# Moving VectorE's side work behind the PSUM sums in a fused modulated-convolution kernel

## The chip, the cores and the metric

The kernel runs on one core of a Trainium2 chip. The metric is the device time of one execution in microseconds (us). The engines are TensorE (PE in the profile; PEld is its weight load), VectorE (DVE), ScalarE (ACT), GpSimd (POOL) and SyncE (SP), which issues the DMAs here. Every engine works through its own instructions in the order in which the program gives them.

## The reference, cut to what matters

A batch of 128 sequences of 64 channels and 1024 positions goes through four modulated 1-D convolutions in a row, with a residual at the end. Each layer has its own style-dependent weights per sample:

```python
TYPES = ('same', 'upsample', 'same', 'downsample')
def _layer(x, style, w, b, mw, mb, typ):
    s = style @ mw.T + mb                                  # (B, 64)
    weight = SCALE * w * s[:, None, :, None]               # per-sample filter, K = 3
    demod = lax.rsqrt(jnp.sum(weight * weight, axis=(2, 3)) + EPS)
    weight = weight * demod[:, :, None, None]
    ...                                                    # conv, bias, blur with [1,3,3,1]
out = x
for i, typ in enumerate(TYPES):
    out = _layer(out, style, weights[i], biases[i], mod_w[i], mod_b[i], typ)
return x + out
```

All four layers are linear in x, so away from the ends of the sequence one sample's result is one convolution with nine taps of 64x64, plus a constant. All data are float32.

## The kernel before, in words

The kernel builds the nine-tap filter of each sample on the chip and applies it once. The 128 partitions hold two samples of 64 channels, a pair p (64 pairs). One iteration q of the main loop handles four samples, the pairs p = 2q and 2q + 1; there are NQ = 32 iterations. The order of all engines' work is written out by hand in this loop, and the semaphores follow from the order in the text.

**Filters.** For the samples of iteration c = q + 2, `stage2(c)` and `stage3(c, 0)`, `stage3(c, 1)` run on TensorE (psR and psW in the profile), and `stage1(q + 3)` (psS) one iteration further ahead. ScalarE copies their results from PSUM, scaled (S, R, Wf, and wd in `scale3`). `combine(c)` on VectorE then makes the filters H from Wf (lines 460 to 473); h1 and h2, complete with line 472, are what the first products of iteration c need.

**Convolution.** The nine taps are applied in three groups of three by a fast filtering scheme: five products m0 to m4 in place of nine. The input of a pair, X, is stored as three planes. From it come five combined inputs, the slots of tile T:
- `pre1(p)`: two VectorE instructions make G from X (lines 499 and 504), and two POOL instructions make T1 and T2 from G (510 and 511); it also issues a load of X;
- `pre2(p)`: `pre2a` makes T3 from X (line 522, VectorE) and issues the other load of X, `pre2b` makes T0 and T4 together from G ("T04", line 532, VectorE).

`convA12(p)` and `convA3(p)` are the products m1, m2 and m3 into PSUM (psA); ScalarE copies m1 out (`copy_m1`, line 573). `seed(p)` consists of `seed1(p)`, the sums u, v and y1, and `seed2(p)`, the two sums that are written into the PSUM banks Y; all are on line 585, read PSUM and run on VectorE. `convB(p)` adds m0 and m4 to Y on TensorE. `output(p, s)` scales Y and y1 into the tile o on ScalarE (line 642), in the last iterations in part on VectorE and POOL (644), and `store(p, s)` sends it off through SP. Y is one pair of banks, so `seed2` of a pair waits until the outputs of the pair before have been read; pairs 61 and 63 have banks of their own (Y2). psA has two buffers.

**Side work.** The three columns at each end of every sequence, and the scale and bias vectors of the samples after the first 16 (`PART[1]`, `REST`), are computed piece by piece alongside. Matrix products of it stand in `SLOTS` (psE, copied to `raw` by ScalarE), the rest in the table `EXTRA`, whose entry (q, 0) belongs to the first half of iteration q and (q, 1) to the second. Most entries are a few short VectorE instructions; (2, 1) is

```python
        (2, 1): lambda: (var_root(REST, after(0)), const_rest(1, PART[1], after(1))),
```

of which `var_root` has an ACT instruction (nw, line 231) and a VectorE one (var, line 232) and `const_rest` two VectorE ones (cc, lines 732 and 733). (2, 0), (4, 1) and (5, 0) are POOL work alone, (3, 0), (4, 0) and (6, 0) have some (lines 270 to 273, 679 to 686). (25, 0) ends with the store of the ends, `out_ends`.

Of the kernel before, what the change touches and what calls it, by code (L numbers as in the profile page):

```python
# [63 lines left out]
def kernel(  # L64
# [12 lines left out]
    NQ = B // 4  # L77
# [86 lines left out]
    def y_bank(p, s):  # L164
        return Y2[p][s] if p in Y2 else Y[:, s]

    def zeros_to_y(sets, n, p=0):


        for i in range(sets):  # L170
            rows = HALF[i % 2]
            for cols in HALF:
                nc.tensor.matmul(
                    y_bank(p, i % 2)[cols, :n], Z[rows, :C], Z[rows, :n], start=True, stop=True
                )
# [53 lines left out]
    def var_root(bs, src, ls=slice(0, NL)):  # L229
        src = by_layer(src, bs)[:, ls]  # L230
        nc_a.activation(nw[:, ls, bs], src, AF.Sqrt, bias=eps)
        nc_v.tensor_scalar(var[:, ls, bs], src, EPS, None, op0=ALU.add)

    def var_inverse(bs, ls=slice(0, NL)):
        nc_v.reciprocal(dm[:, ls, bs], nw[:, ls, bs])
# [14 lines left out]
    def var_newton(bs, ls=slice(0, NL)):  # L250

        newton(var[:, ls, bs], dm[:, ls, bs], nw[:, ls, bs])
# [26 lines left out]
    def table_B(bs):  # L279
        table(nc_g, tB, bs, ALT, DOWN, sc[:, 2, bs], sc[:, 1, bs])  # L280

    def table_0(bs):
        table(nc_g, t0, bs, ALT, ODD, sc[:, 0, bs], 1.0)
# [235 lines left out]
    def pre2a(p, eng=nc_v):  # L519
        if p < NP:  # L520
            X, t = Xs[p % NX], Ts[p]
            eng.tensor_sub(t[:, 4, :NJ], plane(X, 3), plane(X, 1))  # L522
            load(p + NX, slice(1, 3))

    def pre2b(p):
        if p >= NP:
            return
        t, g = Ts[p], Gs.pop(p)

        a, b = plane(g, 2), plane(g, 0)  # L530
        both = lambda v, step: bass.AP(v.tensor, v.offset, [list(v.ap[0]), [step, 2], [1, NJ]])
        nc_v.tensor_sub(t[:, 0:2, :NJ], both(a, PL), both(b, 1))  # L532

    def pre2(p):
        pre2a(p)
        pre2b(p)
# [22 lines left out]
    def m_tile(tag, p, shape=(2, NB)):  # L559
        return mpool.tile([P, *shape], F32, tag=tag, name=f"{tag}_{p}")  # L560
# [23 lines left out]
    def sum_of(out, x, f, y):  # L584
        nc_v.scalar_tensor_tensor(out, x, f, y, op0=ALU.mult, op1=ALU.add)  # L585

    def seed1(p):
        if p >= NP:
            return
        m1, m2, m3 = part.pop(p)  # L590
        u, v = m_tile("u", p), m_tile("v", p)
        y1s[p] = mpool.tile([P, 2, NB], F32, tag="y1", name=f"y1_{p}", bufs=3)
        sum_of(u, m2, -1.0 / 3.0, m1)
        sum_of(v, m2, 1.0 / 3.0, m1)
        sum_of(y1s[p], m3, 2.0 / 6.0, v)
        part[p] = m3, u

    def seed2(p):
        if p >= NP:
            return  # L600
        m3, u = part.pop(p)
        banks = [(slice(s, s + 1), y_bank(p, s)[:, None]) for s in range(2)]
        if p not in Y2:
            banks = [(slice(0, 2), Y)]
        for i, f in enumerate((1.0 / 6.0, 4.0 / 6.0)):
            for k, y in banks:
                sum_of(y[..., i * NB : (i + 1) * NB], m3[:, k], f, u[:, k])

    def seed(p):
        seed1(p)  # L610
        seed2(p)
# [14 lines left out]
    def convB(p, between=None):  # L626
        product(p, 0, [y_bank(p, s)[:, :NB] for s in range(2)])
        if between:
            between()
        product(p, 4, [y_bank(p, s)[:, NB : 2 * NB] for s in range(2)])  # L630
        Ts.pop(p)
        os[p] = opool.tile([P, 2, HO], F32, tag="o", name=f"o{p}")
# [45 lines left out]
    def vector_a1(bs):  # L678
        nc_g.tensor_mul(a1[:, bs], sc[:, 2, bs], sc[:, 1, bs])
# [11 lines left out]
    def vector_b1(bs):  # L691
        with_bias(b1s, sc[:, 2], 1, bs)
# [32 lines left out]
    def const_rest(l, bs, src):  # L725
        src = src[:, : bs.stop - bs.start]
        if l == 2:
            nc_v.tensor_mul(oc[:, bs], src, dm[:, 3, bs])
            nc_v.tensor_scalar(oc[:, bs], oc[:, bs], bb[:, 3:4], None, op0=ALU.add)
        else:  # L730
            add, f = ((b1s, 2.0), (c2f, 1.0))[l]
            nc_v.tensor_mul(cc[l][:, bs], src, (a1, Da)[l][:, bs])
            nc_v.scalar_tensor_tensor(
                cc[l][:, bs], add[:, bs], f, cc[l][:, bs], op0=ALU.mult, op1=ALU.add
            )
# [12 lines left out]
    def zeros():  # L748
        for t in Ye:
            nc_g.memset(t[:, :, 0:1], 0.0)  # L750
            nc_g.memset(t[:, :, 7:8], 0.0)
        for t in Ue:
            nc_g.memset(t[:, :, 0:1], 0.0)
            nc_g.memset(t[:, :, 10:11], 0.0)
        for t in Ve:
            nc_g.memset(t[:, :, 0:2], 0.0)
            nc_g.memset(t[:, :, 10:12], 0.0)
        nc_g.memset(g1, 0.0)
# [255 lines left out]
    def after(side):  # L1014
        return raw[turn[0]][:, side, :]

    def layers(i, j):
        return REST, slice(i, j)


    EXTRA = {
        (1, 1): lambda: const_rest(0, PART[1], after(0)),
        (2, 0): lambda: (table_B(REST), vector_a1(REST)),
        (2, 1): lambda: (var_root(REST, after(0)), const_rest(1, PART[1], after(1))),
        (3, 0): lambda: (var_inverse(*layers(2, 3)), table_0(REST), vector_b1(REST)),
        (3, 1): lambda: (
            const_rest(2, PART[1], after(0)),
            var_newton(*layers(2, 3)),
            var_inverse(*layers(1, 2)),
# [32 lines left out]
        (24, 1): rest3,  # L1062
        (25, 0): rest3_bias,
    }
    for q in range(NQ):
        p = 2 * q
        c, s = q + 2, q + 3
        if q == 1:
            nc.sync.dma_start(Xe, x_ends)
        if q == 5:  # L1070
            zeros()
        if c < NQ:
            stage2(c)
        convB(p)
        output(p, 0)

        if c < NQ:
            stage3(c, 0)
        if q < NQ - 1:
            output(p, 1)  # L1080
        else:
            output(p, 1, nc_v, ((0, 2),))
            output(p, 1, nc_g, ((2, 3),))
            store(p, 0)
            store(p, 1)

            convB(p + 1)
            for i, j, engs in ((2, 3, (nc_a, nc_g)), (0, 2, BOTH)):
                for r, eng in enumerate(engs):
                    output(p + 1, r, eng, ((i, j),))  # L1090
                    store(p + 1, r, slice(i * NB, j * NB))
            break
        convA12(p + 2)
        if q > 2:
            pre1(p + 4)
            store(p, 0)
            seed(p + 1)
            store(p, 1)
            pre2(p + 3)
        elif q:  # L1100

            seed(p + 1)
            pre2(p + 3)
            store(p, 0)
            pre1(p + 4)
            store(p, 1)
        else:
            store(p, 0)
            store(p, 1)
            seed2(p + 1)  # L1110
            var_inverse(PART[1])
            var_newton(PART[1])
            table_A(PART[1], dm[:, 2, PART[1]])
            for of in (table_C, vector_c0, table_3, vector_Da):
                of(PART[1])
            pre2(p + 3)
            pre1(p + 4)
        EXTRA.get((q, 0), lambda: None)()
        if c < NQ:
            stage3(c, 1)  # L1120
        convA3(p + 2)
        if q == NQ - 2:
            convA12(p + 3)
            copy_m1(p + 3)
        side = SLOTS.get(q)
        convB(p + 1, (lambda: slot(*side)) if side else None)
        output(p + 1, 0)
        if q == NQ - 2:
            seed(p + 2)
            convA3(p + 3, lambda p: None)  # L1130
            output(p + 1, 1, nc_v, ((0, 2),))
            output(p + 1, 1, nc_g, ((2, 3),))
            seed_last(p + 3)
        else:
            output(p + 1, 1)
        if c == NQ - 1:

            banks = unit(ps_w, "Y2")
            Y2[p + 3] = Y2[p + 5] = banks
            zeros_to_y(2, 2 * NB, p + 3)  # L1140
        if q > 2 and q < NQ - 2:
            pre1(p + 5)
        if q < NQ - 2:
            seed(p + 2)
        if s < NQ:
            stage1(s)
        if s + 1 < NQ:
            scale3(s + 1)
        if c < NQ:
            combine(c)  # L1150
        pre2(p + 4)
        store(p + 1, 0)
        if q < 3:
            pre1(p + 5)
        store(p + 1, 1)
        EXTRA.get((q, 1), lambda: None)()
        if q < NQ - 2:
            convA12(p + 3)
            convA3(p + 3)
# [74 lines left out]
```

## Time and profile before

| | |
|---|---|
| median of 3 runs | 501.93 us (499.55 to 502.47) |
| own time of the profiled execution | 499.52 us |
| span of the profiled execution | 497.7 us |
| TensorE busy | 486.4 us, 98% of the span |
| VectorE busy | 440.6 us, 89% |
| ScalarE busy | 324.6 us, 65% |
| GpSimd busy | 134.3 us, 27% |

The span runs from the first to the last instruction of the program on the core; the device time of the same execution is 1.8 us longer. A profile's row gives an instruction's line in the kernel, its engine, operation and tiles; a timeline row begins with its start and its duration in us. Ends of matmuls are modelled, and some matmul records are missing after 180 us. One full iteration lasts some 14.4 us, longer where `SLOTS` adds products.

### The profile page before, as it was taken

To read this page: it belongs to the slowest core of one execution; us is meant where nothing else is said; L and a number is where in the kernel's file an instruction comes from. 1 tells how busy PE (TensorE), PEld (TensorE's weight loads), DVE (VectorE), ACT (ScalarE), POOL (GpSimd) and SP (SyncE) were. 2 spreads that over 40 slices of the span, in tenths; PEclk is the share of its full clock that TensorE was granted. 3 is DMA by queue.
4 is the path that set the end of the run, shared out by engine and by line. 5 is a ranking of instruction groups with operands and counts; after the bars stand their busy time and mean duration, and the time that the engine had idled before them with its cause. 6 is when DMAs were issued, how large, how long until landed. Compare 5 with 4: busy or idle time off the path is not lost.

```text
span 497.7 us, 28344 instructions
## 1 busy us (share of the span) xinstructions
PE 486.4 (98%) x12600; PEld 475.7 (96%) x12600; DVE 440.6 (89%) x926; ACT 324.6 (65%) x796; POOL 134.3 (27%) x198
## 2 busy tenths in 40 slices
PE   8999999999999999999999999999999999999985
PEld 5899998999999999999999999999999999999985
DVE  5888989999999889987979998879999889988895
ACT  5456767567767667767667667657667657766642
POOL 4143224254312212212212222212212212221210
PEclk9999999999999999999999999999999999999999
DMA  7132654535554425553435554425555435554223
GB/s 251 61 89 88 212 141 136 153 109 172 164 166 146 141 81 170 172 162 118 135 107 172 168 163 145 150 70 172 173 158 144 139 86 184 172 173 131 92 96 129
DMA packets 37610, 70.81 MB, mean 142 GB/s; under 512 B 4208, under 2 KB 29040, under 8 KB 37488
## 3 DMA queue, kind: packets, MB, share of 16 engines
q1 hardware_dynamic: 37408, 68.88, 44.8%
q8 instruction: 99, 1.62, 1.4%
q14 instruction: 23, 0.19, 0.1%
q10 hardware_dynamic: 80, 0.11, 0.1%
HBM read 35.36 MB, written 33.62 MB: 139 GB/s over the span
## 4 chain that ended last, share of the span: by engine, by line
PE 74%; DVE 3%; ACT 0%; issue 0%
PE psA L550 25%; PE Y L550 18%; PE psR L393 13%; PE psW L430 11%; PE psS L362 5%; PE psE L792 2%; DVE Y L585 1%; ACT o L642 0%; DVE T L532 0%; DVE G L499 0%; DVE v L585 0%; DVE T L522 0%; DVE u L585 0%; DVE o L644 0%; DVE H L472 0%
## 5 line engine op out<-in xcount | busy, mean ns | idle before, releaser
L550 PE MATMUL psA<-T,H 64*64 64x170 f32 x4608 | 207.1, 304 | 2.1 <-DVE Y L585 1.8
L550 PEld LDWEIGHTS psA<-T,H 64*64 64x64 f32 x4608 | 190.2, 133 | 2.7 <-POOL o L644 2.1
L510 POOL TENSOR_TENSOR T<-G 128x342 f32<-128x342 f32 x62 | 56.9, 918 | 319.3 <-DVE G L504 211.5
L550 PE MATMUL Y<-T,Wf 64*64 64x170 f32 x3072 | 141.4, 304 | 1.6 <-DVE Y L585 1.6
L550 PEld LDWEIGHTS Y<-T,Wf 64*64 64x64 f32 x3072 | 128.8, 133 | 3.1 <-ACT m L573 1.4
L642 ACT ACTIVATE o<-Y,oc,dm 128x340 f32<-128x340 f32 x125 | 79.6, 637 | 56.3 <-PE Y L550 56.1
L430 PE MATMUL psW<-R,par 64*64 64x256 f32 (+3 forms) x1536 | 100.1, 349 | 0.0
L585 DVE SCALAR_TENSOR_TENSOR Y<-psA,u 128x340 f32<-128x340 f32 (+1 forms) x132 | 66.5, 508 | 35.9 <-ACT o L642 33.5
L393 PE MATMUL psR<-S,E 64*64 64x192 f32 (+1 forms) x2304 | 94.1, 299 | 1.2 <-DVE S L342 1.0
L340 ACT ACTIVATE Wf<-psW,t 128x256 f32<-128x256 f32 (+1 forms) x252 | 75.5, 382 | 23.1 <-PE psW L430 23.1
L430 PEld LDWEIGHTS psW<-R,par 64*64 64x64 f32 x1536 | 86.0, 133 | 3.0
L393 PEld LDWEIGHTS psR<-S,E 64*64 64x64 f32 x2304 | 86.8, 133 | 1.8 <-DVE S L342 1.3
L340 ACT ACTIVATE R<-psR,tC 128x448 f32<-128x448 f32 x63 | 36.6, 631 | 57.5 <-PE psR L393 54.7
L642 ACT ACTIVATE o<-y,oc,dm 128x170 f32<-128x170 f32 x125 | 65.8, 527 | 0.0
L499 DVE SCALAR_TENSOR_TENSOR G<-X 128x688 f32<-128x688 f32 x64 | 55.7, 871 | 2.3
L511 POOL TENSOR_TENSOR T<-G 128x342 f32<-128x342 f32 x62 | 57.0, 920 | 0.0
L532 DVE TENSOR_TENSOR T<-G 128x684 f32<-128x684 f32 x64 | 55.5, 867 | 0.0
L362 PE MATMUL psS<-wd,par 64*64 64x192 f32 x768 | 46.1, 329 | 0.0
L362 PEld LDWEIGHTS psS<-wd,par 64*64 64x64 f32 x768 | 38.1, 136 | 0.7 <-ACT raw L660 0.3
L573 ACT ACTIVATE m<-psA 128x340 f32<-128x340 f32 x64 | 29.2, 457 | 11.0 <-PE psA L550 7.1
L585 DVE SCALAR_TENSOR_TENSOR y<-psA,v 128x340 f32<-128x340 f32 x64 | 32.7, 512 | 2.2
L585 DVE SCALAR_TENSOR_TENSOR u<-psA,m 128x340 f32<-128x340 f32 x64 | 32.4, 506 | 1.9 <-ACT m L573 1.6
(130 smaller groups left out, 388.6 us busy)
## 6 DMA issues: line engine op xcount, KB each, us to landing
out<-o SPq DMA_DIRECT2D x126, 255.0 KB, 4.1
X<-in_x SPq DMA_DIRECT2D x60, 344.0 KB, 3.4
X<-in_x SPq DMA_DIRECT2D x60, 172.0 KB, 3.2
X<-in_x SPq DMA_DIRECT2D x4, 516.0 KB, 6.4
Xe<-in_x_ends SPq DMA_DIRECT2D x1, 512.0 KB, 5.3
par<-in_params SPq DMA_DIRECT2D x2, 192.0 KB, 3.5
out<-o SPq DMA_DIRECT2D x2, 170.0 KB, 2.9
par_s<-in_params_s SPq DMA_DIRECT2D x1, 196.0 KB, 2.7
```

What stands on the lines that cost most here:

```text
L340: nc_a.activation(dst, src, AF.Copy, scale=f)
L362: nc.tensor.matmul(ps[r][cols, k * C : (k + K) * C], woi[2][rows, k, :], src[rows, :], start=(k == 0), stop=(k == K - 1), skip_group_check ...
L393: nc.tensor.matmul(ps[r][cols, lo * C : (lo + m) * C], E[rows, e + 2, :], src[rows, a, :], start=(n == 0), stop=(n == 8), skip_group_check ...
L430: nc.tensor.matmul(ps[r][cols, (lo - t_lo) * C : (hi - t_lo) * C], woi[0][rows, k, :], rt[c][rows, lo - k : hi - k, :], start=(k == order[0]),
L499: nc_v.scalar_tensor_tensor(g[:, PL:], X[:, : 2 * PL], 0.5, X[:, PL:], op0=ALU.mult, op1=ALU.subtract)
L510: eng.tensor_add(t[:, 2, :NJ], plane(g, 2), plane(g, 1))
L511: eng.tensor_sub(t[:, 3, :NJ], plane(g, 2), plane(g, 1))
L532: nc_v.tensor_sub(t[:, 0:2, :NJ], both(a, PL), both(b, 1))
L550: nc.tensor.matmul(ps[s][cols], w, Ts[p][rows, SLOT[m], j : j + NB], start=(g == 0 and m not in (0, 4)), stop=(g == 2), skip_group_check=True,
L573: nc_a.activation(m1, part[p][0], AF.Copy, scale=-1.0)
L585: nc_v.scalar_tensor_tensor(out, x, f, y, op0=ALU.mult, op1=ALU.add)
L642: nc_a.activation(dst, src, AF.Identity, bias=add, scale=d3)
```

## The change

The entry (q, 0) of `EXTRA` is called between `seed(p + 1)` and `pre2(p + 3)` instead of behind `pre2` (in iterations 1 and 2, where `pre1(p + 4)` follows, also ahead of that). The entry (q, 1) is called right behind `seed(p + 2)`, instead of after `stage1`, `scale3`, `combine`, `pre2(p + 4)` and the stores. A small function `extra` looks the entry up. In iteration NQ - 3 = 29 alone, `pre2(p + 3)` (pair 61) stands between `seed1` and `seed2` of pair 59, and `pre2(p + 4)` (pair 62) stands ahead of `pre1(p + 5)`, the last G (pair 63), instead of behind `combine`. No instruction is added or taken away.

```diff
+    def extra(*at):
+        EXTRA.get(at, lambda: None)()
+
     for q in range(NQ):
...
         if q > 2:
             pre1(p + 4)
             store(p, 0)
+            seed1(p + 1)
+            if q == NQ - 3:
+
+                pre2(p + 3)
+            seed2(p + 1)
+            store(p, 1)
+            extra(q, 0)
+            if q != NQ - 3:
+                pre2(p + 3)
+        elif q:
+
             seed(p + 1)
-            store(p, 1)
-            pre2(p + 3)
-        elif q:
-
-            seed(p + 1)
+            extra(q, 0)
             pre2(p + 3)
             store(p, 0)
             pre1(p + 4)
...
-        EXTRA.get((q, 0), lambda: None)()
...
+        if q == NQ - 3:
+            pre2(p + 4)
         if q > 2 and q < NQ - 2:
             pre1(p + 5)
         if q < NQ - 2:
             seed(p + 2)
+
+        extra(q, 1)
         if s < NQ:
             stage1(s)
         if s + 1 < NQ:
             scale3(s + 1)
         if c < NQ:
             combine(c)
-        pre2(p + 4)
+        if q != NQ - 3:
+            pre2(p + 4)
         store(p + 1, 0)
         if q < 3:
             pre1(p + 5)
         store(p + 1, 1)
-        EXTRA.get((q, 1), lambda: None)()
```

## The prediction

> **What bounds the kernel now.** I read the engine totals first, then the chain that ended last, then TensorE's waits, and last the timelines of VectorE (DVE) and GpSimd (POOL) around those waits. From the page:
>
> ```profile
> span 497.7 us, 28344 instructions
> PE 486.4 (98%) x12600; PEld 475.7 (96%) x12600; DVE 440.6 (89%) x926; ACT 324.6 (65%) x796; POOL 134.3 (27%) x198
> ...
> PE 74%; DVE 3%; ACT 0%; issue 0%
> ```
>
> TensorE is busy 98% of the span, so an order on VectorE is worth only the time in which TensorE stands still for VectorE. All such time after the start-up is in the waits of TensorE (columns: total us, times, longest):
>
> ```profile
> PE psA L550 <- DVE Y L585: 1.8, 1, 1.8
> PE Y L550 <- DVE Y L585: 1.6, 2, 1.1
> ```
>
> In its timeline these are three places: 1.09 us ahead of the product that starts at 87.42 us, 0.54 at 117.33, and 1.78 at 484.24. A matmul normally starts before its predecessor's modelled end, so I count from start to start: 86.03 to 87.42, 101.85 to 102.16 (a third, shorter stop), 116.49 to 117.33 and 482.16 to 484.24, less a normal 0.04 each: 1.35 + 0.27 + 0.80 + 2.04 = 4.5 us. That is the ceiling. Between 117 and 482 us TensorE never waits 0.3 us for anything.
>
> **The stretch from 76 to 117 us.** Iteration 2 starts it. VectorE has no idle time over 0.1 us from 75.34 to 117.19, where the sums Y that release 117.33 end, so each microsecond taken out there moves 87.42 and 117.33 alike. What runs ahead of 87.42:
>
> ```profile
> 80.38 0.87 DVE L499 SCALAR_TENSOR_TENSOR G<-X 128x688 f32<-128x688 f32 x1
> 81.17 0.51 DVE L504 SCALAR_TENSOR_TENSOR G<-X 128x342 f32<-128x342 f32 x1
> 81.59 0.36 DVE L232 TENSOR_SCALAR var<-raw 128x384 f32<-128x384 f32 x1
> 81.86 0.93 DVE L732 TENSOR_TENSOR cc<-raw,Da 128x16 f32<-128x16 f32 x1
> 82.82 0.84 DVE L733 SCALAR_TENSOR_TENSOR cc<-c2f,cc 128x16 f32<-128x16 f32 x1
> 83.59 0.86 DVE L499 SCALAR_TENSOR_TENSOR G<-X 128x688 f32<-128x688 f32 x1
> 84.37 0.50 DVE L504 SCALAR_TENSOR_TENSOR G<-X 128x342 f32<-128x342 f32 x1
> 84.80 0.50 DVE L585 SCALAR_TENSOR_TENSOR u<-psA,m 128x340 f32<-128x340 f32 x1
> ```
>
> The two cc of 16 columns take 0.93 and 0.84 us; the same lines took 0.17 each at 66.41. Beside them POOL does the two T:
>
> ```profile
> 81.82 0.93 POOL L510 TENSOR_TENSOR T<-G 128x342 f32<-128x342 f32 x1 [5.64 <-DVE G L504]
> 82.71 0.92 POOL L511 TENSOR_TENSOR T<-G 128x342 f32<-128x342 f32 x1
> ```
>
> Each cc ends 0.04 us after one of them (82.79 after 82.75, 83.67 after 83.63): a VectorE instruction with two tensors in SBUF stood until POOL's ended. The sums on line 585, which read PSUM, run beside POOL at their usual 0.50.
>
> **The edit "side work behind the sums", iteration 2.** EXTRA(2,1) is now ahead of combine and pre2, where POOL is idle. Start to start the trio takes 0.27 + 0.21 + 0.09 = 0.57 us (81.59 to 81.86 in the rows above; 66.41 to 66.62 to 66.71 for the cc) instead of 2.00 (81.59 to 83.59). It moves the G at 80.38 to 80.95. But the cc had also kept the next G, that of pre1(10), off POOL's T. Now this G comes straight behind, at 82.16, and its first part runs to 82.16 + 0.87 = 83.03. POOL's first T, ready at 81.82 + 0.57 = 82.39, waits for that, and ends at 83.03 + 0.92 = 83.95. G's second part stands until then. How long after such a wait an instruction ends, line 468 shows: at 35.42 it took 0.78 us instead of 0.55 and ended (36.20) 0.42 after POOL's T (35.78). So 83.95 + 0.42 = 84.37, and u starts 0.08 before that, at 84.29 instead of 84.80: **0.5 us gained**. That the two engines take turns rests on the rows at 105.42 to 106.86: POOL's c0f, waiting since 105.58, ended at 106.49, after the first part of G (106.29), and G's second part took 0.66 instead of 0.51. Bounds: if POOL's second T also goes ahead of G's second part, 0.92 more, a loss of 0.4; if G's second part is not held at all, it ends at 83.46 and the gain is 1.4. I take 0.5, the reading of the nearest rows.
>
> **The same edit in the other iterations.** The order of side work and T between two sums changes, not the amount, so no sum gets earlier or later; what gets later is what is put behind.
> - Combine stands behind EXTRA(q,1). Its h2 is done 3.3 us ahead of the product that needs it in iteration 3 (95.05 against 98.35), where the side work is longest: 96.64 to 98.41, 1.8 us. In iteration 5 it is 3.7 against 1.2, later at least 2.6 against at most 1.4. Hidden by over 1 us everywhere; without that cover each overrun goes into TensorE whole.
> - T3 and T04 of pre2(p+3) stand behind EXTRA(q,0). The longest is (4,0), 103.12 to 105.42, 2.3 us. T3 is done 2.46 us before convA12(11) starts at 104.88, and convA3 needs it 1.7 later: 4.2 against 2.3. Nothing.
> - POOL's side work: only (2,0) passes POOL's T. tB and a (74.83 to 76.18) move into POOL's idle time behind 68.46, beside PSUM sums. Nothing.
> - ACT: nw (0.62 us at 77.14) goes ahead of the two S of stage1, which ended at 76.56 and are needed at 77.01. They end near 77.06, plus about 0.1 for the signal: TensorE stops some 0.2 us. It then arrives 0.2 later at the stop of 1.35, where it would wait anyway. Nothing.
> - SP: the loads of pre2(p+3) are issued up to 2.3 us later, four X buffers ahead of use; the out_ends store passes one load that waits for a later VectorE instruction anyway. Nothing.
>
> **The edit in iteration 29.** Here the order before:
>
> ```profile
> 469.60 0.51 DVE L585 SCALAR_TENSOR_TENSOR y<-psA,v 128x340 f32<-128x340 f32 x1
> 471.21 1.07 DVE L585 SCALAR_TENSOR_TENSOR Y<-psA,u 128x340 f32<-128x340 f32 x2 [1.09 <-ACT o L642]
> 472.19 0.51 DVE L522 TENSOR_TENSOR T<-X 128x342 f32<-128x342 f32 x1
> 472.62 0.87 DVE L532 TENSOR_TENSOR T<-G 128x684 f32<-128x684 f32 x1
> 473.57 0.88 DVE L499 SCALAR_TENSOR_TENSOR G<-X 128x688 f32<-128x688 f32 x1
> ...
> 480.45 0.51 DVE L522 TENSOR_TENSOR T<-X 128x342 f32<-128x342 f32 x1
> 480.87 0.87 DVE L532 TENSOR_TENSOR T<-G 128x684 f32<-128x684 f32 x1
> 481.65 0.51 DVE L585 SCALAR_TENSOR_TENSOR u<-psA,m 128x340 f32<-128x340 f32 x1
> ```
>
> Pre2(61) goes into the 1.09 us of idle time ahead of Y; pre2(62) goes from 480.45 to the place that becomes free at 472.2. Sums(61) then follow combine directly: 481.65 - 480.45 = 1.20 us earlier, and with them the product at 484.24 (stopped 2.04). Against this: pre2(61) starts at 470.04, while POOL's last T runs 469.77 to 470.69. By the row of line 468 its T3 ends at 470.69 + 0.42 = 471.11, T04 at 471.9, the two Y at 472.9 instead of 472.29: 0.6 late. TensorE wanted them at 472.64; Y to product takes 0.14 (484.10 to 484.24), so product 0 of pair 59 starts at 473.03, 0.39 late. The outputs of 59, Y of 60 (476.61, released by ACT) and combine follow by 0.39. Net 1.20 - 0.39: **0.8 us gained**. Bounds: 1.2 if POOL does not hold T3, 0.6 if TensorE loses the whole 0.6. From 484.24 on TensorE runs without a stop up to 0.3 us at 490.52, so the end moves with it.
>
> Here a rule of the Trainium skill speaks against the edit: "SBUF — State Buffer", section "Who interferes with whom", says that a VectorE instruction with two SBUF inputs and a reading GpSimd instruction exclude each other, and the second to issue blocks fully. The trace has a row that looks otherwise: G at 9.96 took its usual 0.86 us beside a POOL row that lasted from 9.81 to 11.34. By the rule T3 is held and the change is worth 1.3 us, by that row it is not and the change is worth 1.7.
>
> **Sum.** 0.5 + 0.8 = 1.3 us off a span of 497.7: 496.4. The profiled execution's own time was 499.52, 1.8 above its span, so 498.2 like for like. The median of the three runs shown is 501.93, 2.4 above that execution, so I put the forecast at 501.93 - 1.3 = 500.6.
>
> **Rivals.**
> - *Nothing moves*: the gain at iteration 2 goes back into G behind T (loss 0.4) and the tail gives its low 0.6. 501.7. For it: that side work had served as a spacer. Against it: the rows of turn-taking. Chance 0.25.
> - *More than I count*: G is not held (1.4), T3 is not held (1.2), and the shift also takes what is left of the stops, 4.5 in all at most. 497.4 to 499.3. For it: the row at 9.96. Against it: line 468, 35.42. Chance 0.18.
> - *Slower: combine becomes late.* If the filters are needed earlier than the psA rows show, every EXTRA(q,1) holds TensorE by its overrun. The fifteen that hold VectorE work sum to about 13 us (1.8 in iteration 3, 1.4 in 19, 0.3 to 1.2 in the others). It decides from the point at which the margin of about 3.3 falls under the side work's length; with no margin 501.9 + 13 = 515, with half of it 508. Against it: the margins counted above. Chance 0.05.
> - My forecast, 0.52: 499.0 to 502 with the spread of the runs.
>
> **How the numbers follow.** One per cent, 5.0 us, is about what a measurement of this kernel can tell from no change. The ceiling of 4.5 is below that, so faster by over 1% takes luck with the runs: 0.03. Slower by over 1% is the third rival, 0.05. The range: the lowest run, 499.55, less both good ends (2.6) gives 497.0; the highest, 502.47, plus the bad end of iteration 2 (0.4) gives 502.9. The runs' own spread of 2.9 is most of it.
>
> **What would show it.** Right: the cc of (2,1) at 0.17 each, straight behind Y near 76.4; the second part of the G that now follows near 82.2 longer than 0.51; the stop ahead of 87.42 down from 1.09 to about 0.6; T3 of pair 61 longer than 0.51; the stop of 1.78 down to about 0.5 to 0.7. Wrong: a new wait of TensorE between 117 and 470 us, above all psA on DVE H, or a G of pre1(10) that stands for both T.

## The result, and the profile after

The changed kernel takes 499.84 us (median of 20 runs, 497.88 to 502.26), the kernel before 501.05 in its 20 runs on the same chip (499.34 to 502.47). The ratio is 0.9974, with a 95% interval of 0.9961 to 0.9986: by this ratio **1.3 us faster**, a quarter of one per cent (the two medians are 1.2 apart). The forecast was 500.6, and 1.3 us of gain. It started from the median of three runs, 501.93, which is 0.9 above that of the 20 runs; from 501.05 the same gain would have given 499.75. The gain came out; its two terms did not, and what follows is mostly about them.

The head of the page, its chain of work that ended last, and TensorE's waits (total us, times, longest):

```profile
span 498.0 us, 28356 instructions
PE 487.5 (98%) x12600; PEld 476.5 (96%) x12600; DVE 441.9 (89%) x926; ACT 324.7 (65%) x796; POOL 134.3 (27%) x198
...
PE 96%; DMA 1%; SPq 1%; ACT 1%; DVE 1%; issue 0%; ACTq 0%
```

```profile
PE Y L550 <- ACT m L573: 0.7, 1, 0.7
PE psA L550 <- ACT m L573: 0.6, 1, 0.6
PE psA L550 <- issue: 0.3, 1, 0.3
```

The chain could be followed back over 77% of the span before, and over nearly all of it now; VectorE's share of it went from 3% to 1%. The two waits of 1.8 and 1.6 us on VectorE's sums are gone from the table, and two of 0.7 and 0.6 us stand in their place. These two, at 118.64 and 484.38 us, are still ended by the sums Y, 0.15 and 0.14 us after their ends (118.49, 484.24), as before (0.14). The view names a copy m of ScalarE because that ended a little later. But before, the product now at 118.64 started (117.33) while that copy was still running (116.97 to 117.44), so it does not wait for it; the copy near 484 reads the other psA buffer. Here the column is not to be taken at its word. The rows that answer to those of iterations 2 and 29 stand with the steps below.

Yet this profiled execution's span is not shorter than the one before: 498.0 against 497.7, and its own time 499.74 against 499.52. The difference lies ahead of anything that was changed. The clock that TensorE was granted, in windows of 2 us (the last columns are clock, DMA share, GB/s), before:

```profile
13.00:15.00 2.00, 2.00 (x68) 2.00 (x64) 1.37 (x5) 0.00 (x0) 0.73 (x3) 1.00 0.11 34
15.00:17.00 2.00, 2.00 (x35) 1.63 (x28) 1.39 (x3) 0.64 (x1) 1.18 (x7) 1.00 0.58 176
```

and after:

```profile
13.00:15.00 2.00, 2.00 (x32) 2.00 (x34) 1.46 (x5) 0.00 (x0) 0.65 (x3) 0.50 0.12 41
15.00:17.00 2.00, 2.00 (x48) 1.96 (x45) 0.00 (x0) 0.00 (x0) 1.27 (x7) 0.75 0.62 169
```

The first copy m of the main loop starts at 27.64 us before and at 29.26 after, 1.6 us later. The same dip came in six of the ten profiles of this study, whatever the kernel, so I compare profiles from that copy to the end of the span and call this **the loop**: 470.1 us before, 468.7 after, 1.4 less, which agrees with the ratio of the runs.

Within the loop, TensorE's stops from start to start, as in the prediction (the trace before holds all 12600 of TensorE's products, behind 180 us too, so that no stop in it is a missing record):

| stop of TensorE at (us of before) | 87 | 102 | 117 | 484 |
|---|---|---|---|---|
| before | 1.39 | 0.31 | 0.84 | 2.09 |
| after | none | 0.38 | 1.01 | 0.88 |

One more stop of 0.63 (77.43 to 78.06) has no releaser in the trace after and none like it before; the last section says what it looks like. Up to 118 us the account is, less the normal 0.04 each: 1.35 + 0.27 + 0.80 = 2.42 before, and 0.34 + 0.97 + 0.59 plus 0.22 by which the copy m at 73 us is already late (43.92 us after the first one instead of 43.70) = 2.12 after. So the stretch up to there gave 0.3 us, and the stop near 484 the other 1.2.

### The profile page after: what moved, and what is told of

Read it like the earlier page. It is cut to its first block, busy times and chain, and to the rows that moved or that the text cites. A ratio compares the mean times of both kernels' runs of the same rounds, so it can differ in the third digit from the quotient of the medians.

```text
span 498.0 us, 28356 instructions
## 1 busy us (share of the span) xinstructions
PE 487.5 (98%) x12600; PEld 476.5 (96%) x12600; DVE 441.9 (89%) x926; ACT 324.7 (65%) x796; POOL 134.3 (27%) x198
## 4 chain that ended last, share of the span: by engine, by line
PE 96%; DMA 1%; SPq 1%; ACT 1%; DVE 1%; issue 0%; ACTq 0%
PE psA L550 33%; PE Y L550 22%; PE psR L393 17%; PE psW L430 15%; PE psS L362 7%; PE psE L792 2%; DMA X<-in_x 1%; SPq L111 0%; PE Y L173 0%; SPq L110 0%; ACT R L340 0%; ACT m L573 0%; ACT Wf L340 0%; DVE G L499 0%; DVE o L644 0%
## 5 line engine op out<-in xcount | busy, mean ns | idle before, releaser
L393 PE MATMUL psR<-S,E 64*64 64x192 f32 (+1 forms) x2304 | 95.4, 302 | 2.0 <-DVE S L342 1.7
L393 PEld LDWEIGHTS psR<-S,E 64*64 64x64 f32 x2304 | 88.0, 135 | 2.6 <-DVE S L342 2.0
L362 PE MATMUL psS<-wd,par 64*64 64x192 f32 x768 | 45.1, 326 | 0.0
L573 ACT ACTIVATE m<-psA 128x340 f32<-128x340 f32 x64 | 29.1, 455 | 10.5 <-PE psA L550 6.8
```

The lines of the kernel that those rows point to most:

```text
L362: nc.tensor.matmul(ps[r][cols, k * C : (k + K) * C], woi[2][rows, k, :], src[rows, :], start=(k == 0), stop=(k == K - 1), skip_group_check ...
L393: nc.tensor.matmul(ps[r][cols, lo * C : (lo + m) * C], E[rows, e + 2, :], src[rows, a, :], start=(n == 0), stop=(n == 8), skip_group_check ...
L573: nc_a.activation(m1, part[p][0], AF.Copy, scale=-1.0)
```

## The experiments

Each has the computation of the reference whole. In the first four, the table `EXTRA` is read at its new place for the entries in a set `EARLY` and at its old place for the others. Chain offsets below are starts of VectorE's sums u or ends of its sums Y, counted from the first copy m, against the same ones before.

**The two halves.** `tail_only` keeps all side work at the old places and has both edits of iteration 29; `side_only` moves all side work and leaves iteration 29 as it was.

```diff
 # tail_only
+    EARLY = []
 # side_only
+    EARLY = [(q, h) for q in range(NQ) for h in range(2)]
-            if q == NQ - 3:
-                pre2(p + 3)
...
-        if q == NQ - 3:
-            pre2(p + 4)
```

> The two edits of iteration 29 alone, all side work at its old places. Theory A (two parts, read from the two profiles: 1.2 us from the tail, 0.3 from the side work): 1.2 us faster than the kernel before, the stop ahead of the first product of pair 63 down from 2.09 to 0.9 us start to start, the stops near 87, 102 and 117 us as before (1.4, 0.3, 0.8). Rival B (the side work brings all of it): no gain, the tail's stop smaller but the time lost elsewhere.

> All side work behind the sums, iteration 29 as before. Theory A: 0.3 us faster than the kernel before, stop near 87 us gone, that near 117 us about 1.0 instead of 0.8, the one near 484 still 2.1. Rival B: 1.3 us faster.

Measured, `tail_only`: 499.07 us against 500.75, ratio 0.9970 (0.9952 to 0.9988); the stop near 484 is 0.89. Measured, `side_only`: 500.71 against 500.75, ratio 0.9996 (0.9981 to 1.0011); the stop near 87 is gone, those near 102 and 117 are 0.98 and 1.01 (0.31 and 0.84 before), that near 484 is 2.09. So nearly all that the times can show comes from iteration 29. The side work gives 0.36 us by the chain of VectorE (the end of the sums Y that release the stop near 117), which its interval can't tell from nothing. One thing came otherwise than expected: in `tail_only`, whose side work is where it was, the stop near 87 is 0.57 and not 1.4, because TensorE had already lost 0.63 us at 75.79, in a stop without a releaser like the one at 77.43. It reaches the late sums later and waits for them less.

**Which of the side work.** `only_2_1` moves the one entry (2, 1), `all_but_2_1` every entry but that one; both leave iteration 29 as before.

```diff
 # only_2_1
+    EARLY = [(2, 1)]
 # all_but_2_1
+    EARLY = [(q, h) for q in range(NQ) for h in range(2) if (q, h) != (2, 1)]
```

> Of all side work only entry (2, 1) moves, iteration 29 as before. Theory A, with its second half (a G that follows T04 at once waits for it, since it takes the G buffer that T04 has just read; the side work in the old place hid that): (2, 1) alone gains 1.0 to 1.4 us, more than all the side work together (0.3), since the G of iterations 3 and 4 start behind side work again. Rival C (the other entries cost nothing, the gain of (2, 1) is only what TensorE can use): 0.3 us as with all entries. By B 1.3.

> All side work but entry (2, 1) moves, iteration 29 as before. Theory A: slower than before by 0.4 to 0.7 us (three G of iterations 3 and 4 that now wait for T04, some 0.17 to 0.24 each, in the stretch where VectorE sets the pace); cc of (2, 1) at 0.9 and 0.8 us as before. Rival C: no difference.

Measured: 500.38, ratio 0.9988 (0.9973 to 1.0003), and 501.81, ratio 1.0014 (0.9998 to 1.0031). The times point the expected ways, but both intervals include 1, no change; the chain gives the sizes. In `only_2_1` the sums u that follow pre1(10) start 1.43 us earlier, counted from the sums before; by the next sums u 0.97 of it is lost again. VectorE and then POOL there, from their timelines:

```profile
86.85 1.06 DVE L585 SCALAR_TENSOR_TENSOR Y<-psA,u 128x340 f32<-128x340 f32 x2
87.83 0.64 DVE L522 TENSOR_TENSOR T<-X 128x342 f32<-128x342 f32 x1
88.39 1.58 DVE L532 TENSOR_TENSOR T<-G 128x684 f32<-128x684 f32 x1
```

```profile
84.48 1.84 POOL L510 TENSOR_TENSOR T<-G 128x342 f32<-128x342 f32 x1 [6.22 <-DVE G L504]
86.28 0.92 POOL L511 TENSOR_TENSOR T<-G 128x342 f32<-128x342 f32 x1
87.17 0.91 POOL L510 TENSOR_TENSOR T<-G 128x342 f32<-128x342 f32 x1
88.05 1.18 POOL L511 TENSOR_TENSOR T<-G 128x342 f32<-128x342 f32 x1
89.21 1.37 POOL L270 TENSOR_SCALAR t<-sc 64x48 f32<-64x48 f32 x2
```

T04 takes 1.58 us instead of 0.87: it stands while POOL still works off the T that came in late. That is 0.68 of the 0.97; T3 ahead of it costs 0.14, and the G behind it 0.15, beside POOL's b1s. The expectation had the right gain at pre1(10) but no such second collision: by the sums Y near 117 about 0.5 us of the 1.43 is left, not 1.0 to 1.4. The stops that remain are 0.99 near 103 us and 0.84 near 118. In `all_but_2_1` the two cc are as long as ever (0.93 and 0.85), and the chain loses 0.55 us by the sums near 117: three steps of 0.17 to 0.19, each at a place where the moved side work no longer stands between T04 and the next G.

The times of these four kernels can be read more finely with the clock that TensorE was granted in each run. In the 35 runs of the kernel before that stand beside them, 11 with a mean granted clock of 0.998 or more average 499.5 us, the other 24 average 501.25. With a straight line for this, the same for both kernels (0.41 to 0.45 us for 0.001 of clock), `tail_only` comes out 1.1 us faster than the kernel before (give or take 0.3), `side_only` 0.2 faster (0.3), `only_2_1` 0.45 faster (0.24) and `all_but_2_1` 0.7 slower (0.3). This is an estimate from those runs; it has the sizes that the chain has.

**The two edits of iteration 29, one at a time.** `t61` moves only pre2(61) between the sums, `t62` only pre2(62) ahead of the last G; all side work is at the old places.

```diff
 # t61: without the move of pre2(62)
-        if q == NQ - 3:
-            pre2(p + 4)
...
+        pre2(p + 4)
 # t62: without the move of pre2(61)
-            if q == NQ - 3:
-                pre2(p + 3)
...
+            pre2(p + 3)
```

> Of the change only pre2(61) between the two parts of the sums of pair 59; all else as before. Theory D (the tail's gain is pre2(62) leaving the place between combine and the sums of 61; pre2(61) in the idle time only keeps that from being paid at Y of 60): no gain, the stop ahead of the first product of pair 63 stays at 2.1 us, T3 of pair 61 takes about 1.0 us because POOL's last T still runs. Rival E (filling the idle time is itself the gain): that stop falls by up to 1.1.

> Of the change only pre2(62) ahead of the last G; all else as before. Theory D: G of 63 and the sums of 60 come 1.2 us later, Y of 60 about 0.7 later since 0.35 us of idle time and some slack take a part, so of the 1.2 about 0.5 is left: the stop ahead of pair 63's first product falls from 2.1 to about 1.5 us, and TensorE gets a new stop of about 0.6 ahead of product 0 of pair 60. Rival E: no gain without the filled idle time.

Measured in one profile each (single times of 499.23 and 500.97 us, too few to compare, the second with the dip of the clock). `t61`: the stop near 87 is 0.60 and not 1.4, as in `tail_only` and for the same reason (0.60 lost at 75.70); the stop near 484 is still 2.08 and the copies m of pairs 62 and 63 are 3.75 us apart as before; T3 is held as it is with the whole change, and TensorE loses nothing by it:

```profile
469.97 1.04 DVE L522 TENSOR_TENSOR T<-X 128x342 f32<-128x342 f32 x1
470.93 0.86 DVE L532 TENSOR_TENSOR T<-G 128x684 f32<-128x684 f32 x1
471.71 1.06 DVE L585 SCALAR_TENSOR_TENSOR Y<-psA,u 128x340 f32<-128x340 f32 x2
```

`t62`: those copies are 2.55 apart, 1.20 less, and a new stop of 0.58 appears ahead of product 0 of pair 60, at 480.75. Its sums Y then follow pre2(61), pre2(62) and G without the idle time that had stood there: 

```profile
474.54 0.51 DVE L522 TENSOR_TENSOR T<-X 128x342 f32<-128x342 f32 x1
474.96 0.87 DVE L532 TENSOR_TENSOR T<-G 128x684 f32<-128x684 f32 x1
475.74 0.51 DVE L522 TENSOR_TENSOR T<-X 128x342 f32<-128x342 f32 x1
476.16 0.86 DVE L532 TENSOR_TENSOR T<-G 128x684 f32<-128x684 f32 x1
476.94 0.87 DVE L499 SCALAR_TENSOR_TENSOR G<-X 128x688 f32<-128x688 f32 x1
...
479.54 1.06 DVE L585 SCALAR_TENSOR_TENSOR Y<-psA,u 128x340 f32<-128x340 f32 x2
```

The last stop was 0.90 and not the 1.5 that I expected, since TensorE itself arrives there some 0.55 late. So the move of pre2(62) brings all of the 1.20 us, and the move of pre2(61) brings nothing alone but keeps about 0.55 of it from being lost.

**A third G buffer.** If the G behind T04 pays because it reuses the buffer that T04 is reading, another buffer takes the cost away.

```diff
-tc.tile_pool(name="gpool", bufs=2)
+tc.tile_pool(name="gpool", bufs=3)
```

> The changed kernel with three G buffers instead of two. Theory F (each G that follows T04 directly waits some 0.17 us for it, because it takes the buffer that T04 reads): on VectorE, the 0.09 us of idle time ahead of those G goes, the sums of pair 11 come 0.5 to 0.7 us earlier than in the changed kernel, the stop near 117 us falls from 1.0 to 0.3 or 0.4, and the time by 0.5 to 0.7: about 1.9 faster than the kernel before. Rival G (the wait is for something else, X or a T buffer): no difference from the changed kernel, 1.3 faster than before.

Measured: 499.14 us against 501.00, ratio 0.9955 (0.9939 to 0.9972). After, with two buffers:

```profile
88.83 0.89 DVE L532 TENSOR_TENSOR T<-G 128x684 f32<-128x684 f32 x1
89.81 0.88 DVE L499 SCALAR_TENSOR_TENSOR G<-X 128x688 f32<-128x688 f32 x1
```

and with three:

```profile
89.25 0.89 DVE L532 TENSOR_TENSOR T<-G 128x684 f32<-128x684 f32 x1
90.06 0.89 DVE L499 SCALAR_TENSOR_TENSOR G<-X 128x688 f32<-128x688 f32 x1
```

With two, G starts 0.09 us after T04's end; with three, 0.08 before it. That is the 0.17 of each step. The page's group of all 64 G shows the same (last number: idle time of the engine just before them), first after, then with three buffers:

```profile
L499 DVE SCALAR_TENSOR_TENSOR G<-X 128x688 f32<-128x688 f32 x64 | 56.0, 875 | 4.7
```

```profile
L499 DVE SCALAR_TENSOR_TENSOR G<-X 128x688 f32<-128x688 f32 x64 | 55.6, 868 | 0.0
```

Before the change it was half of that:

```profile
L499 DVE SCALAR_TENSOR_TENSOR G<-X 128x688 f32<-128x688 f32 x64 | 55.7, 871 | 2.3
```

The third buffer takes it all away. Behind 118 us this idle time costs nothing, since TensorE does not wait there. The stop near 117 falls from 1.01 to 0.64, and the chain from Y of iteration 2 to Y near 117 is 0.67 us shorter than after. The times of the two kernels alone do not tell them apart (0.9955 and 0.9974, with intervals that overlap); the rows do.

**One G earlier as well.** The last kernel adds to this the first half of what iterations 3 and on do anyway: in iteration 2, pre1 of the pair p + 5 stands ahead of the sums, not behind combine, so that only one G follows pre2 there.

```diff
-        if q > 2 and q < NQ - 2:
+        if q > 1 and q < NQ - 2:
             pre1(p + 5)
...
-        if q < 3:
+        if q < 2:
             pre1(p + 5)
```

> As the one with three G buffers, and in iteration 2 pre1(9) stands ahead of the sums of pair 6, where VectorE sat idle 1.05 us before Y, instead of behind combine. Theory H (what the moved entry (2, 1) won was given back half because POOL's two T of pair 9 came late and met the G of pair 10, T3 and T04): POOL's T run beside the sums, VectorE's chain to the sums of pair 11 gets another 1 us or more earlier, no stop near 117 us, about 2.5 to 3.4 us faster than the kernel before. Rival: the T of pair 9 wait for TensorE to free their buffer and hold the side work of (2, 1) instead; no more than the three buffers alone, 1.9.

Measured: 498.07 us against 501.00, ratio 0.9948 (0.9927 to 0.9969), some 2.6 us by the ratio and the best version here, though its interval meets that of the changed kernel at 0.9961 to 0.9969. Its loop is 467.4 us. The stop near 117 is 0.42, where I had expected none. The G that was moved now stands in a tighter place, where POOL gets in between its two parts:

```profile
72.95 0.87 DVE L499 SCALAR_TENSOR_TENSOR G<-X 128x688 f32<-128x688 f32 x1
73.74 1.24 DVE L504 SCALAR_TENSOR_TENSOR G<-X 128x342 f32<-128x342 f32 x1
```

```profile
73.18 1.43 POOL L510 TENSOR_TENSOR T<-G 128x342 f32<-128x342 f32 x1 [3.00 <-DVE G L504]
74.57 1.19 POOL L511 TENSOR_TENSOR T<-G 128x342 f32<-128x342 f32 x1
```

## Why the prediction was right, and where it was not

**Iteration 2, gain of 0.5: the step failed in which POOL's first T waits for the first part of G only, and "G's second part stands until then".** The cc came out as predicted, 0.17 each behind Y. But G was not held at all, POOL was:

```profile
78.25 0.17 DVE L732 TENSOR_TENSOR cc<-raw,Da 128x16 f32<-128x16 f32 x1
78.46 0.17 DVE L733 SCALAR_TENSOR_TENSOR cc<-c2f,cc 128x16 f32<-128x16 f32 x1
...
83.82 0.87 DVE L499 SCALAR_TENSOR_TENSOR G<-X 128x688 f32<-128x688 f32 x1
84.61 0.51 DVE L504 SCALAR_TENSOR_TENSOR G<-X 128x342 f32<-128x342 f32 x1
85.03 0.51 DVE L585 SCALAR_TENSOR_TENSOR u<-psA,m 128x340 f32<-128x340 f32 x1
```

```profile
84.06 1.85 POOL L510 TENSOR_TENSOR T<-G 128x342 f32<-128x342 f32 x1 [7.55 <-PE Y L550]
85.86 0.94 POOL L511 TENSOR_TENSOR T<-G 128x342 f32<-128x342 f32 x1
```

POOL's T, ready at 84.06, stood through both parts of G (to 85.12) and ended 0.79 us later, while both G rows keep their usual 0.87 and 0.51. The good bound of the prediction, 1.4, was the right value: u starts 1.39 us earlier than before. The row that I had taken as the nearest one (G's second part at 0.66, beside c0f) was a real row, and the last experiment shows the turn-taking again, with a G of 1.24; but in the changed kernel, in `side_only`, in `only_2_1` and with three buffers POOL's T took 1.84 or 1.85. What decides between the two outcomes I can't say: in both, POOL became ready about 0.23 us after the start of G's first part.

**The other iterations, where the order was to change, "not the amount, so no sum gets earlier or later": this step failed.** Two prices were missing. One is what POOL's late work does next: in `only_2_1` it holds T3 and T04 of pair 9 and the G behind them for 0.97 us, in `side_only` T3 takes 0.85 instead of 0.51, in the whole change POOL's b1s holds the second part of a G to 0.66. The other is the wait of G for T04 over the shared buffer, 0.17 us three times, which side work at its old place had filled. The chain of VectorE after the change, against before, in the order of time: 1.39 us earlier at u of iteration 2; 1.00 at the end of the sums Y after it, which now wait 0.31 us for ScalarE's o, and so for TensorE; 0.66 at the next u (0.17 for the buffer, 0.15 for b1s); 0.49 and 0.32 at the two after that (0.17 each); 0.32 at the Y that release the stop near 117. Net 0.32, not 0.5.

The stops read well once this is known. The one near 87 disappears, and those near 102 and 117 grow by 0.07 and 0.17: an engine that stops less at one place reaches the next late sum earlier and waits for it there. What counts is the chain at the last of these stops, 0.32 us. The sign "down from 1.09 to about 0.6" for the stop near 87 was wrong because G was not held.

**Things costed at nothing that were nothing.** Combine: no new stop of TensorE on VectorE between 118 and 470 us, so the rival of the late combine had no ground. ScalarE's nw ahead of the two S: in `side_only`, where TensorE is not late for another reason there, the psR products at that place end 51.88 us after the first copy m instead of 51.77, and the next stop takes this 0.11 up, as the prediction had it. In the changed kernel TensorE comes there 0.8 us late, by the 0.22 and the stop at 77.43, so that nw costs it nothing.

**The tail, gain of 0.8: the mis-sized term is the "0.39 late" of TensorE at pair 59; it measured 0.** The hold of T3 came as foreseen:

```profile
471.37 1.03 DVE L522 TENSOR_TENSOR T<-X 128x342 f32<-128x342 f32 x1
472.32 0.86 DVE L532 TENSOR_TENSOR T<-G 128x684 f32<-128x684 f32 x1
473.10 1.06 DVE L585 SCALAR_TENSOR_TENSOR Y<-psA,u 128x340 f32<-128x340 f32 x2
...
477.95 1.08 DVE L585 SCALAR_TENSOR_TENSOR Y<-psA,u 128x340 f32<-128x340 f32 x2
...
481.79 0.51 DVE L585 SCALAR_TENSOR_TENSOR u<-psA,m 128x340 f32<-128x340 f32 x1
```

```profile
471.11 0.92 POOL L511 TENSOR_TENSOR T<-G 128x342 f32<-128x342 f32 x1
```

T3 takes 1.03 instead of 0.51 and ends 0.37 after POOL's T (472.40, 472.03). This is the rule of the Trainium skill ("SBUF — State Buffer", section "Who interferes with whom") that spoke against the edit; here the trace agrees with it. Nor does the row at 9.96 speak against it: by the rows, what stood there was POOL. Its row from 9.81 to 11.34 is one of four alike instructions (t on line 270, 64x8) and took 1.53 us, the other three 0.28, 0.47 and 0.37; it ends 0.10 after the second part of that G (11.24). The trace before thus had a row in which POOL stands through both parts of a G, the outcome that iteration 2 then gave. Y ends at 474.16, later than it would have by some 0.5 us. But TensorE comes to it without a stop: in its timeline the last group of psA runs until the first Y products begin at 474.31:

```profile
473.50 1.07 PE L550 MATMUL psA<-T,H 64*64 64x170 f32 x19
474.31 0.76 PE L550 MATMUL Y<-T,Wf 64*64 64x170 f32 x13
```

In the trace before I had read "TensorE wanted them at 472.64" from the first of a few Y products that were recorded among those of psA; the last product of psA began at 472.93:

```profile
472.64 0.30 PE L550 MATMUL Y<-T,Wf 64*64 64x170 f32 x1
...
472.93 0.30 PE L550 MATMUL psA<-T,H 64*64 64x170 f32 x1
```

The true need was 472.97, so there were 0.33 us more of slack than I counted. Thus the tail gives its whole 1.20: the copies m of pairs 62 and 63 are 2.55 us apart instead of 3.75, and the stop falls from 2.09 to 0.88. In the wait table, in which the prediction had it at 1.78, it is now 0.6: the sign "about 0.5 to 0.7" came true, but it could not tell a gain of 1.2 from one of 0.8, since 0.39 would have made TensorE and the sums late alike and left the same stop.

**The sum.** By the loops of the two profiles: 0.32 from the side work and 1.20 from the tail are 1.5, measured 1.4 there and 1.3 by the ratio of the runs. Predicted 0.5 and 0.8. Three errors (a gain of 0.9 not counted in iteration 2, a loss of about 1.1 behind it, a loss of 0.4 in the tail that did not come) mostly cancelled: that the sum came out is luck, and the forecast time was better than its reasons.

## What to carry to other kernels

When an instruction moves out of a tight stretch of the engine that sets the pace, follow what the other engine on the same operands then does late, through the next few stops: here 1.4 us won at one place kept only 0.3 two iterations on. Short work that stands between two instructions with a buffer in common may be filling a wait; taking it away shows the wait (0.17 us each), and one more buffer took it away here. Read when a matmul engine needs something from the last product ahead of it, not from the first record of the group that uses it. And before two profiles are compared place by place, find the stops that the change did not bring or take away: a stop without a releaser ahead of a late sum makes the wait for that sum look shorter.

## What the runs showed of the hardware that I had not expected

- **The start-up of TensorE varies by about 1.6 us between executions of the same code.** In six of ten profiles the granted clock fell to between 0.50 and 0.78 in windows from 13 to 17 us; the first copy m then came at 29.1 to 29.4 us, without the dip at 27.6 to 27.8. The dip follows the wait for ScalarE's and VectorE's S (1.66 us without a product ahead of 12.82 in the profile after, 0.97 ahead of 12.73 before), but in the last experiment a wait of 2.1 us brought none, so the wait's length alone does not decide. The runs fit this: by the averages given with the experiments (499.5 and 501.25), those with the higher mean clock are 1.8 us faster, about half of the spread of some 3 us and more than the change is worth.
- **TensorE stops now and then for 0.4 to 0.9 us with no releaser in the trace, and these stops look like waits for its own instructions.** There are twelve of them, in nine of the ten profiles, near 63, from 75 to 79, at 94 or near 432 us (77.43 to 78.06 after, 432.64 to 433.20 in `all_but_2_1`), and none in the profile before. All twelve end at a TensorE record (products, weight loads and sequencer records, in order of start) whose number from 0 is 193 plus a multiple of 256. The page of the kernel after has a queue named instruction (transfers, MB, share of time):

```profile
q8 instruction: 99, 1.62, 1.4%
```

Its 99 transfers of 16,384 bytes make one for every 256 or 257 of the 25,432 records. Each stop ends 1.28 to 1.57 us after the transfer of that number has landed (in the profile after at 76.73, the product at 78.06), and at none of the some 980 such places in the ten profiles does TensorE go on sooner than 1.28 after it. In the profile before, the place of the 77-us stop has its transfer 3.04 us ahead, and no stop. Place and timing speak for waits for code; no run varied the code's place, and what makes a transfer late stays open. Such a stop shortens the wait at the next late sum, as near 87 us in `tail_only`. Behind the ones near 432 us in `side_only` (0.83) and `all_but_2_1` (0.56) the stop near 484 is 2.09 as before, so those two profiles are longer by them.
- **Which of VectorE and POOL goes first** when one waits and the other has two instructions in a row came out both ways (T of 1.85 beside an untouched G; T of 1.43 and G of 1.24), with the same timing of the two at the start.
